# Attention scores with keys on partitions, two heads on halves of the array, no maximum, and a checked fallback

## Chip, cores, metric

One Trainium2 chip, one core. The time is device microseconds of the whole program, from the first to the last instruction; every figure called a time is a median of runs on the chip. TensorE's granted clock is told by the profile.

## The reference, cut to what matters

```python
# x: (32, 512, 512) float32, adj: (512, 512) float32 of 0 and 1, with ones on the diagonal
def L0(x, adj, Wq, bq, Wk, bk, Wv, bv):            # H = 8 heads of HD = 64
    q, k, v = [(x @ W + b).reshape(b_, n, H, HD) for W, b in ...]
    scores = einsum('bihd,bjhd->bhij', q, k) / sqrt(64)
    scores = scores + where(adj == 0, -1e9, 0)
    return einsum('bhij,bjhd->bihd', softmax(scores, axis=-1), v)
def L1(x, adj, weight, bias):                      # d = rsqrt of the degrees
    return einsum('nm,bmo->bno', adj * d[:, None] * d[None, :], x @ weight) + bias
x = layernorm(x + L0(x, ...));  x = layernorm(x + L1(x, ...))
```

So there are 32 graphs of 512 nodes, each with 8 heads. Everything stays float32.

## The kernel before

Queries and keys are made transposed, two heads in each block of 128 partitions. Scores have queries on partitions; the softmax's weights are then turned on TensorE for the product with the values. Cuts are marked.

```python
    def scores(s):
        b, i, h = s                                   # graph, 128 queries, head
        r = slice((h % 2) * HD, (h % 2 + 1) * HD)
        p = ps_sc.tile([P, N], F32, name="sc")
        nc.tensor.matmul(p, QT[b][r, h // 2, ts(i, P)], KT[b][r, h // 2, :], start=True, stop=True)
        # ... neg = -(p + mask), low = its minimum (VectorE, one instruction)
        nc.scalar.activation(E[s], neg, AF.Exp, bias=low, scale=-1.0, accum_out=SUMS[b, i][:, h : h + 1])

    def turn(s):
        for j in range(NT):
            nc.tensor.transpose(p[:, j, :], e[:, ts(j, P)], ident)
        # ... to SBUF on VectorE or ScalarE in turn

    def values(s):
        for j in range(NT):
            nc.tensor.matmul(av[:, h, :], et[:, j, :], V[b][:, j, ts(h, HD)], start=j == 0, stop=j == NT - 1)
        # ... after the last head: 1 / sums, weighting, residual, layer norm

    for k in range(S + 3):
        # ... scores(k), turn(k - 2), values(k - 3); all of project(b + 1) at once in mid-graph,
        #     all of convolve(b - 1) at once at step 8
```

`project` and `convolve` are 12 and 8 pieces a graph, each of four float32 products with 512 columns; I call these 20 the pieces.

## Time and profile before

| | before |
|---|---|
| time, median (lowest to highest) | 4829.75 us (4829.08 to 4830.41) |
| TensorE busy, granted clock | 99.6% of the span, 0.999 |
| VectorE, ScalarE, GpSimd busy | 35%, 29%, 10% |
| TensorE instructions | 19,984 matmul instructions (two to a float32 product, one to a transpose) and as many weight loads |

TensorE is busy from end to end, so time can only be won by fewer or shorter TensorE slots. A slot is the distance between starts; recorded durations overlap. The profile's lines are in the prediction below. In them PE is TensorE, PEld its weight loads, DVE VectorE, ACT ScalarE and POOL GpSimd; L157 is line 157 of the kernel; a line of the groups view ends with the busy us, the mean ns of one, and the idle us ahead of it with its cause.

### The profile page before, as it was taken

The numbers are of one execution on the slowest core, as the hardware profiler recorded it, in microseconds if no ns is written. First come the engines' busy times: TensorE is split into PE (matmuls) and PEld (weight loads), VectorE is DVE, ScalarE is ACT, GpSimd is POOL, SyncE is SP. The second block draws the span as 40 slices with busy tenths as digits, with TensorE's granted clock in tenths as the row PEclk, the third lists the DMA queues.
The fourth block names the chain that finished last, engine by engine and source line by source line (L and its number), as shares of the span: only waits on it lengthen the run. The fifth ranks groups of instructions, "written<-read, shape, count | busy, mean of one in ns | idle before, by whom it ended". The sixth has DMA issues, their size and how long they took to land.

```text
span 4827.6 us, 50352 instructions
## 1 busy us (share of the span) xinstructions
PE 4808.6 (100%) x19984; PEld 2717.6 (56%) x19984; DVE 1700.5 (35%) x4110; ACT 1402.3 (29%) x3073; POOL 462.8 (10%) x520
## 2 busy tenths in 40 slices
PE   9999999999999999999999999999999999999999
PEld 4555555555555555555555555555555555555555
DVE  2433334333343333433334333343333433334334
ACT  2232233322333222332223232232322323223232
POOL 0100101000010100101001010010000110101101
PEclk9999999999999999999999999999999999999999
DMA  1000000000000000000000000000000000000000
GB/s 66 18 10 9 18 18 18 10 9 18 18 18 9 12 16 18 18 9 18 9 18 18 9 18 9 18 18 9 18 9 18 18 9 18 9 18 18 9 9 18
DMA packets 38009, 76.10 MB, mean 16 GB/s; under 512 B 2192, under 2 KB 2192, under 8 KB 37776
## 3 DMA queue, kind: packets, MB, share of 16 engines
q1 hardware_dynamic: 37776, 72.88, 4.2%
q8 instruction: 159, 2.61, 0.2%
q14 instruction: 74, 0.61, 0.0%
HBM read 39.33 MB, written 33.55 MB: 15 GB/s over the span
## 4 chain that ended last, share of the span: by engine, by line
PE 99%; DMA 0%; DVE 0%; POOL 0%; issue 0%; SPq 0%; POOLq 0%
PE sc L157 22%; PE mm L142 18%; PE av L199 18%; PE tr L174 12%; PE mm L229 9%; PE mm L147 9%; PE mm L221 9%; PE mm L133 1%; DMA wk<-in_L_gnn_Wk_dram 0%; PE mm L122 0%; DVE st L183 0%; POOL y L210 0%; DVE y L231 0%; DVE y L207 0%; POOLq L290 0%
## 5 line engine op out<-in xcount | busy, mean ns | idle before, releaser
L157 PE MATMUL sc<-kT,qT 64*128 64x512 f32 x2048 | 1149.3, 641 | 0.0
L160 DVE CUSTOM_DVE_ANT_0 neg<-sc,mask 128x512 f32<-128x512 f32 x1024 | 707.8, 691 | 973.9 <-PE sc L157 969.1
L199 PE MATMUL av<-v,eT 128*128 128x64 f32 x8192 | 1027.4, 268 | 0.0
L199 PEld LDWEIGHTS av<-v,eT 128*128 128x128 f32 x8192 | 995.5, 192 | 1.0 <-issue 0.7
L166 ACT ACTIVATE e<-neg,low 128x512 f32<-128x512 f32 x1024 | 740.7, 723 | 767.8 <-DVE low L160 767.6
L174 PEld LDWEIGHTS tr<-ident,e 128*128 128x128 f32 x4096 | 432.9, 141 | 767.6 <-ACT e L166 655.8
L179 ACT COPY eT<-tr 128x512 f32<-128x512 f32 x512 | 299.6, 585 | 1506.9 <-PE tr L174 1506.9
L174 PE MATMUL tr<-ident,e 128*128 128x128 f32 x4096 | 675.5, 286 | 0.0
L148 DVE TENSOR_TENSOR v<-mm,bv_r 128x512 f32<-128x512 f32 x128 | 88.5, 692 | 1266.9 <-PE mm L147 1266.9
L210 POOL TENSOR_TENSOR y<-y,x 128x512 f32<-128x512 f32 x128 | 162.2, 1268 | 3293.6 <-DVE y L207 2811.6
L142 PE MATMUL mm<-xT,wk 128*128 128x512 f32 x1024 | 449.7, 597 | 3.3 <-DMA wk<-in_L_gnn_Wk_dram 2.6
L221 PE MATMUL mm<-naT,x 128*128 128x512 f32 x1024 | 447.2, 594 | 1.0 <-DVE x L190 1.0
L142 PE MATMUL mm<-xT,wq 128*128 128x512 f32 x1024 | 444.7, 592 | 0.0
L147 PE MATMUL mm<-wv,xT 128*128 128x512 f32 x1024 | 444.7, 592 | 0.0
L229 PE MATMUL mm<-w,zT 128*128 128x512 f32 x1024 | 444.7, 592 | 0.0
L157 PEld LDWEIGHTS sc<-kT,qT 64*128 64x128 f32 x2048 | 301.4, 184 | 93.7 <-issue 29.3
L177 DVE COPY eT<-tr 128x512 f32<-128x512 f32 x512 | 349.6, 683 | 2.1 <-PE tr L174 2.1
L147 PEld LDWEIGHTS mm<-wv,xT 128*128 128x128 f32 x1024 | 194.6, 190 | 244.9 <-issue 244.9
L229 PEld LDWEIGHTS mm<-w,zT 128*128 128x128 f32 x1024 | 194.6, 190 | 244.9 <-issue 244.9
L142 PEld LDWEIGHTS mm<-xT,wq 128*128 128x128 f32 x1024 | 194.6, 190 | 244.9 <-issue 244.9
L142 PEld LDWEIGHTS mm<-xT,wk 128*128 128x128 f32 x1024 | 192.5, 190 | 241.5 <-issue 225.9
L221 PEld LDWEIGHTS mm<-naT,x 128*128 128x128 f32 x1024 | 191.8, 190 | 230.2 <-issue 227.7
(37 smaller groups left out, 1649.4 us busy)
## 6 DMA issues: line engine op xcount, KB each, us to landing
x<-in_x_dram SPq DMA_DIRECT2D x32, 1024.0 KB, 5.1
out_dram<-ob SPq DMA_DIRECT2D x32, 1024.0 KB, 4.2
wq<-in_L_gnn_Wq_dram SPq DMA_DIRECT2D x1, 1024.0 KB, 7.8
wk<-in_L_gnn_Wk_dram SPq DMA_DIRECT2D x1, 1024.0 KB, 10.4
wv<-in_L_gnn_Wv_dram SPq DMA_DIRECT2D x1, 1024.0 KB, 9.5
ob<-in_adj_dram SPq DMA_DIRECT2D x1, 1024.0 KB, 8.9
w<-in_L_gnn_weight_dram SPq DMA_DIRECT2D x1, 1024.0 KB, 11.0
bv_r<-in_L_gnn_bv_dram SPq DMA_DIRECT2D x1, 256.0 KB, 7.4
```

The source lines that it names most:

```text
L142: nc.tensor.matmul(p, w[:, d, ts(o, P)], xT[:, d, :], start=d == 0, stop=d == DT - 1)
L147: nc.tensor.matmul(p, xT[:, d, ts(n, P)], wv[:, d, :], start=d == 0, stop=d == DT - 1)
L157: nc.tensor.matmul(p, QT[b][r, h // 2, ts(i, P)], KT[b][r, h // 2, :], start=True, stop=True)
L160: nc.vector.tensor_tensor_reduce(neg, p, mask[:, i, :], scale=-1.0, scalar=3.4028234663852886e38, op0=ALU.add, op1=ALU.min, accum_out=low)
L166: nc.scalar.activation(E[s], neg, AF.Exp, bias=low, scale=-1.0, accum_out=SUMS[b, i][:, h : h + 1])
L174: nc.tensor.transpose(p[:, j, :], e[:, ts(j, P)], ident)
L177: nc.vector.tensor_copy(ET[s], p)
L179: nc.scalar.copy(ET[s], p)
L199: nc.tensor.matmul(av[:, h, :], et[:, j, :], V[b][:, j, ts(h, HD)], start=j == 0, stop=j == NT - 1)
L210: nc.gpsimd.tensor_add(y, y, X[b][:, i, :])
L221: nc.tensor.matmul(p, x1[:, m, ts(d, P)], naT[:, m, :], start=m == 0, stop=m == NT - 1)
L229: nc.tensor.matmul(p, zT[:, d, ts(n, P)], w1[:, d, :], start=d == 0, stop=d == DT - 1)
```

## The change

The intent: with the keys on partitions the exponentials come out as the values product wants them, so the 4096 transposes go. The values (64 columns) become the stationary side and the weights stream 512 columns at a time. The two heads of a block are issued as neighbours, on TensorE rows 0-63 and 64-127 for the scores and on columns 0-63 and 64-127 for values and sums, so that the two halves of the array may work at once. The maximum is dropped; the mask becomes a factor of 0 or 1. A running sum of totals and reciprocals on GpSimd is tested at the end, and a complete general path stands behind a branch (not taken here). Projections and convolutions are handed out in pieces between the attention's groups. A group is two heads of a graph, all 512 queries: 128 groups, four to a graph.

```diff
-    def scores(s):
-        ...
-        nc.tensor.matmul(p, QT[b][r, h // 2, ts(i, P)], KT[b][r, h // 2, :], start=True, stop=True)
-        ... tensor_tensor_reduce (add mask, minimum), exp with bias=low and accum_out
-    def turn(s): ... (four transposes and a copy for each head and 128 queries)
+    def scores(g, j):
+        b, q = divmod(g, NP)
+        p = ps_sc.tile([P, 2, N], F32, name="sc")
+        for u in range(2):
+            r = slice(u * HD, (u + 1) * HD)
+            nc.tensor.matmul(p[:, u, :], KT[b][r, q, ts(j, P)], QT[b][r, q, :], start=True, stop=True)
+        e = work.tile([P, 2, N], F32, name="e", bufs=2 * NT)
+        nc.scalar.activation(e, p, AF.Exp, scale=SCALE)
+        nc.vector.tensor_mul(e, e, maskT[:, j, None, :].to_broadcast([P, 2, N]))
+        ... total of the four e's on VectorE
+    def values(g):
+        for j in range(NT):
+            e = E.pop((g, j))
+            for u in range(2):
+                nc.tensor.matmul(p[u * HD : (u + 1) * HD, :], V[b][:, j, ts(2 * q + u, HD)], e[:, u, :],
+                                 start=j == 0, stop=j == NT - 1)
+        for u in range(2):
+            nc.tensor.matmul(s[u * HD : (u + 1) * HD, :], ones, total[:, u, :], start=True, stop=True)
+        nc.gpsimd.tensor_add(seen_total, seen_total, total)
+        nc.vector.reciprocal(r, s)
+        nc.gpsimd.tensor_add(seen_recip, seen_recip, r)
+        nc.vector.tensor_mul(OT[g], p, r)
+    def residual(g): ... four transposes of OT[g], added to x; after the last group the layer norm
+    for g in range(G + 1):
+        ... scores(g, 0), scores(g, 1), values(g - 1), scores(g, 2), scores(g, 3)
+        for k in range(max(n_project, n_convolve)):
+            if k < n_project:
+                projecting.pop(0)()
+            if k < n_convolve:
+                convolving.pop(0)()
+        ... residual(g - 1)
```

(Cut: the general path, the mask's transposes, the layer norm over four tiles at once, the test and branch at the end.)

## The prediction

> **What bounds the kernel now.** I read the page first (busy table, chain that ended last, groups), then the timeline of TensorE over some microseconds in the middle, then the groups by line for the small VectorE operations.
>
> ```profile
> PE 4808.6 (100%) x19984; PEld 2717.6 (56%) x19984; DVE 1700.5 (35%) x4110; ACT 1402.3 (29%) x3073; POOL 462.8 (10%) x520
> ...
> PE 99%; DMA 0%; DVE 0%; POOL 0%; issue 0%; SPq 0%; POOLq 0%
> PE sc L157 22%; PE mm L142 18%; PE av L199 18%; PE tr L174 12%; PE mm L229 9%; PE mm L147 9%; PE mm L221 9%; PE mm L133 1%; DMA wk<-in_L_gnn_Wk_dram 0%; PE mm L122 0%; DVE st L183 0%; POOL y L210 0%; DVE y L231 0%; DVE y L207 0%; POOLq L290 0%
> ...
> L157 PE MATMUL sc<-kT,qT 64*128 64x512 f32 x2048 | 1149.3, 641 | 0.0
> ...
> L199 PE MATMUL av<-v,eT 128*128 128x64 f32 x8192 | 1027.4, 268 | 0.0
> ...
> L174 PE MATMUL tr<-ident,e 128*128 128x128 f32 x4096 | 675.5, 286 | 0.0
> ...
> L142 PE MATMUL mm<-xT,wq 128*128 128x512 f32 x1024 | 444.7, 592 | 0.0
> ```
>
> TensorE does everything: 99% of the chain, no idle time ahead of any matmul group. So the time is a sum of TensorE slots. One float32 product is two instructions (L142 has 512 products and 1024 instructions), and the slot of an instruction with 512 columns is 444.7/1024 = 0.434 us, although its recorded duration is 592 ns (records overlap). A product with 512 columns costs 0.868 us.
>
> The timeline gives the slots of an attention step (one head, 128 queries), from start to start:
>
> ```profile
> 2400.82 1.12 PE L157 MATMUL sc<-kT,qT 64*128 64x512 f32 x2
> 2401.88 0.66 PE L174 MATMUL tr<-ident,e 128*128 128x128 f32 x4
> 2402.37 1.00 PE L199 MATMUL av<-v,eT 128*128 128x64 f32 x8
> 2403.30 1.12 PE L157 MATMUL sc<-kT,qT 64*128 64x512 f32 x2
> ```
>
> Scores 1.06, turning the weights 0.49, values 0.93, together 2.48 us. With 1024 steps that is 2540 us; 20 pieces of projection and convolution for each of 32 graphs, 8 instructions each, are 20 x 32 x 3.47 = 2222; turning x (L133) 70. The sum is 4832 against a span of 4827.6, so this account is complete. Two things stand out. A scores product takes 1.06 us where two slots of a full product are 0.87: 0.19 us a step are lost at the change between 64 rows and 128. And the values stream 64 columns for each load of 128 weights: 0.116 us for each of 8 pairs, where 64 columns at the rate of L142 are 0.054. They are bound by weight loads.
>
> The other engines matter only for what comes after:
>
> ```profile
> L166 ACT ACTIVATE e<-neg,low 128x512 f32<-128x512 f32 x1024 | 740.7, 723 | 767.8 <-DVE low L160 767.6
> ...
> L210 POOL TENSOR_TENSOR y<-y,x 128x512 f32<-128x512 f32 x128 | 162.2, 1268 | 3293.6 <-DVE y L207 2811.6 <-issue 482.0
> L207 DVE TENSOR_TENSOR y<-av,inv 128x512 f32<-128x512 f32 x128 | 88.5, 692 | 94.3 <-PE av L199 94.3
> ...
> L222 ACT COPY zT<-mm 128x512 f32<-128x512 f32 x128 | 74.9, 585 | 381.7 <-PE mm L221 381.7
> ...
> L205 DVE RECIPROCAL inv<-sums 128x8 f32<-128x8 f32 x128 | 26.0, 203 | 35.8 <-ACT e L166 35.8
> ...
> L116 DVE TENSOR_TENSOR dis<-root,pos 128x4 f32<-128x4 f32 x1 | 0.2, 165 | 1.2 <-POOL root L114 1.2
> ```
>
> **What the Trainium skill says.** (1) "TensorEngine Tiling (Array Packing)", Key Properties: tiles of the array work independently, but changing the tiling mode drains TensorE. The trace agrees with the second half (the 0.19 us above); the first half it can't show, since no two products on different halves are neighbours in it. (2) "TensorE: Matmul & The Clock Gate", Part 3, measured speedup: four row tiles gave 3.07x and three column tiles 2.38x at 512 columns, and matmuls start and end in program order. Nothing says that this held for float32, and no trace here shows it. (3) "VectorE: DVE Perf Modes", the section on the TRN2 errata: a float32 tensor_tensor takes (N+151)/0.96 ns. For N = 512 this is 691, the trace has 692; for 1024 I get an estimate of 1.22 us. (4) "SBUF — State Buffer", Who interferes with whom: VectorE and GpSimd share a port pair as an exclusive lock. No view of before shows a case; afterwards GpSimd adds while VectorE multiplies.
>
> **The change part by part.** The unit is a group: two heads of one graph, all 512 queries; 4 groups a graph, 128 in all.
>
> Removed: all 4096 transposes of weights with their 1024 evacuations, the maximum on VectorE, and values products with only 64 columns. Now the values are the stationary side (64 columns) and the weights stream, 512 columns at a time. The count of scores products stays 1024.
>
> Scores: 8 products a group, in two bursts of four, alternately on rows 0-63 and 64-127 and into different banks. Call the instructions of a burst A1 A2 B1 B2 A1' A2' B1' B2'. As the order is kept and each half does one at a time, A2 runs beside B1, B2 beside A1' and so on: 5 slots instead of 8. With one drain at 0.19: 2 x (5 x 0.434 + 0.19) = 4.72 us.
>
> Values: 8 products on alternating column halves, then 2 products with ones that give the sums already spread over 64 partitions: 20 instructions in 11 slots: 11 x 0.434 + 0.19 = 4.96 us. (Unpaired the sums alone would cost 256 x 0.868 = 222 us.)
>
> Turning the output back: 4 transposes a group, 0.55 us (L133: 69.6/128 = 0.54). Turning x: the same, 0.55. Unchanged: 5 pieces a group, 5 x 3.47 = 17.36 us.
>
> Sum: 4.72 + 4.96 + 0.55 + 0.55 + 17.36 = 28.14 us; x 128 = **3602 us**.
>
> Beside it, for each group: ScalarE has 4 exponentials of 1024 columns, under 2 x 0.585 = 1.17 us each, and 3 evacuations of about 0.65: some 6.6 us. VectorE has 7 operations on 1024 columns (4 masks, 3 additions) x 1.22 = 8.6; a reciprocal on 512 columns; four operations of 0.69 (weighting, residual, v, convolution) = 2.8; and two layer norms a graph, 5.9 each or 2.9 a group (4 x (0.695 + 0.176 + 0.547), + 0.15). The reciprocal is slow: 203 ns for 8 elements, where an ordinary operation on 4 takes 165, or 161 without its 4 x 1.04 ns; (203 - 161)/8 = 5.25 ns an element, 512 x 5.25 + 161 = 2.85 us, which is drawn from a very small case, so 2.4 to 4.4. Sum 8.6 + 2.9 + 2.8 + 2.9 = 17.2 us, 61% of the group. GpSimd: 2.5 + 1.3 + 1.3 us, estimated from 1268 ns for 512 columns, about 5 us. Each is below TensorE, so it stays the bound on average.
>
> Waits I add. The short iteration is the first of a graph: only x is turned in it, so TensorE has 4.7 + 5.0 + 2.2 + 0.6 = 12.5 us of work, while VectorE has about 11.5 us up to the finished output of the previous group plus masks and the layer norm behind it. The transposes of x also need evacuations on ScalarE behind two exponentials. I take 1.5 us there, and 1.7 us in the later iterations where v and the convolution are evacuated behind VectorE's queue of masks: 3.2 x 32 = about 100 us. At the ends: the last group has nothing to fill its chain (sums, reciprocal, weighting, transpose, residual, layer norm, about 11 us), then comes the convolution's own norm, and the new check with its branch; before, all idle time was 19 us. I add 45. **3602 + 100 + 45 = about 3750 us.**
>
> **The rivals.** *No overlap of float32 halves.* Each product keeps 0.868: scores 2 x (4 x 0.868 + 0.19) = 7.32, values and sums 10 x 0.868 + 0.19 = 8.87, the rest 18.46: 34.65 x 128 = 4435, with about 100 for waits and ends 4540. For it: nothing here shows float32 pairs side by side. Against: row halves read disjoint partitions, and the instructions' order allows it. *Only row halves overlap* (column halves need two streams of moving data from the same partitions): 4.72 + 8.87 + 18.46 = 32.05, x 128 = 4102, with waits 4220. *Only column halves*: 7.32 + 4.96 + 18.46 = 30.74, 3935, with waits 4055. *VectorE becomes the bound*: if the shared port blocks it for the 5 us of GpSimd and the reciprocal takes 4.4, its group is 24 us, still under 28, but bursts would show: 6 to 8 us a graph, 200 us more, about 3900. *Each mode change is dearer*, as there are now about four a group: at 0.4 us each instead of 0.57 in all it would be +130 us.
>
> **Range and chances.** I give full overlap 0.65 (3600 to 3950 with its waits), row alone 0.13, column alone 0.05, none 0.12, and 0.05 to surprises such as a longer slot in tiled modes. Even without any overlap the sum is 6% below 4830, so faster by over 2% is 0.96, within 2% 0.03, slower 0.01. The range 3560 to 4240 holds full overlap and most of row overlap; the middle is the full-overlap sum.
>
> **What would show it.** Scores in the groups view: about 2 x 5 x 0.434 x 128 = 556 us of TensorE busy time (889 if not paired), and starts a few ns apart for A2 and B1. Values and sums together about 611 us (1111 if not). Pieces still 0.434 us an instruction. Exponentials near 1.1 us, masks 1.22, reciprocal 2.4 to 4.4. The chain should stay over 93% TensorE, with the rest naming VectorE in each graph's first iteration. The prediction is wrong if paired products start 0.43 us apart all through, if TensorE idles over 8% behind VectorE, or if the tiled slots are longer than 0.434.

## The result

3758.42 us (3757.99 to 3760.56, 4 runs) against 4829.75; ratio 0.7783, 95% interval 0.7772 to 0.7794. All outputs are right. Ratios are the mean time of one kernel's fast runs over that of the other's of the same rounds, so not quite the ratio of the medians quoted. The predicted 3750 is within 0.3%. The experiments show that this closeness is partly luck: two terms of the sum were off by 4 to 5 us a graph each, in opposite directions.

The page of the changed kernel, busy times first and then the groups that answer to those of before (busy us, mean ns | idle ahead of them and its cause):

```profile
PE 3537.8 (94%) x10786; PEld 1471.0 (39%) x10786; DVE 2297.7 (61%) x2390; ACT 817.7 (22%) x1025; POOL 825.8 (22%) x459
...
L294 ACT ACTIVATE e<-sc 128x1024 f32<-128x1024 f32 x512 | 499.9, 1022 | 1325.9 <-PE sc L292 1325.9
L295 DVE TENSOR_TENSOR e<-e,maskT 128x1024 f32<-128x1024 f32 x512 | 698.3, 1385 | 128.9 <-ACT e L294 128.9
L322 POOL TENSOR_TENSOR seen_recip<-seen_recip,recip 128x512 f32<-128x512 f32 x128 | 263.6, 2059 | 2091.1 <-DVE recip L321 1842.8
L363 PE MATMUL mm<-naT,x 128*128 128x512 f32 x1024 | 538.6, 676 | 185.5 <-DVE x L338 185.5
L292 PE MATMUL sc<-qT,kT 64*128 64x512 f32 x2048 | 554.1, 618 | 0.8 <-ACT e L294 0.8
L311 PE MATMUL av<-e,v 128*64 128x512 f32 x2048 | 467.7, 598 | 0.0
L321 DVE RECIPROCAL recip<-su 128x512 f32<-128x512 f32 x128 | 428.6, 3349 | 60.2 <-PE su L318 60.2
L264 PE MATMUL mm<-xT,wk 128*128 128x512 f32 x1024 | 464.9, 598 | 0.0
```

There are about half as many TensorE instructions (54%), and 2048 scores instructions of 512 columns take 554 us instead of 1149. TensorE is no longer full: one group, the convolution's gather L363, has 185.5 us of idle time ahead of it, all for VectorE's last step of the layer norm (L338); and its own instructions are busy 538.6 us where the like-sized L264 have 464.9. The chain that ended last cannot be used here: it stops at the branch at the end and names less than 1% of the span.

The timeline of TensorE shows a graph's first two groups (start us, busy us, line, how many):

```profile
2000.31 1.99 PE L292 MATMUL sc<-qT,kT 64*128 64x512 f32 x8
2002.22 3.65 PE L311 MATMUL av<-e,v 128*64 128x512 f32 x16
2005.71 1.03 PE L318 MATMUL su<-total,ones 128*64 128x512 f32 x4
...
2009.61 1.12 PE L292 MATMUL sc<-qT,kT 64*128 64x512 f32 x2
...
2020.74 3.70 PE L264 MATMUL mm<-xT,wk 128*128 128x512 f32 x8
2030.33 6.04 PE L363 MATMUL mm<-naT,x 128*128 128x512 f32 x8 [5.89 <-DVE x L338]
2036.20 3.60 PE L264 MATMUL mm<-xT,wk 128*128 128x512 f32 x8
```

From start to start a scores burst of 8 instructions takes 1.91 us and the 16 of the values 3.49, which is 8 slots of 0.436: two instructions to a slot. The starts in the trace's records say the same (us, first six instructions of the scores burst): 2000.307, 2000.314, 2000.840, 2000.847, 2001.270, 2001.276. Pairs start 7 ns apart. At 2030.33 the bracket shows the wait of 5.89 us, and the eight gather instructions after it take 5.87 us to the next start instead of 3.43. The table of stretches tells why:

```profile
2013.32:2030.33 17.01, 11.12 (x41) 3.77 (x41) 14.84 (x19) 4.20 (x5) 5.46 (x3) 0.94 0.00 0
2030.33:2036.20 5.87, 5.87 (x8) 2.56 (x9) 5.84 (x8) 0.00 (x0) 0.00 (x0) 0.60 0.00 0
2053.90:2086.84 32.94, 32.94 (x97) 13.78 (x96) 18.44 (x16) 7.21 (x10) 10.39 (x6) 1.00 0.00 0
```

Columns are the stretch, its length, busy time (count) of TensorE, weight loads, VectorE, ScalarE and GpSimd, then the granted clock, DMA share and GB/s. The clock is 0.60 in the gather after the wait, and 1.00 in a group without one. In the clock records the half-speed interval comes once in each graph that has such a wait and lasts 6.8 us.

What VectorE and GpSimd did before that gather, in the same window:

```profile
2016.34 3.07 DVE L295 TENSOR_TENSOR e<-e,maskT 128x1024 f32<-128x1024 f32 x1
...
2023.13 3.32 DVE L321 RECIPROCAL recip<-su 128x512 f32<-128x512 f32 x1
2026.37 0.10 DVE L334 TENSOR_SCALAR ve<-mv 128x4 f32<-128x4 f32 x1
...
2029.73 1.92 DVE L338 TENSOR_SCALAR x<-x,mv,rstd 128x512 f32<-128x512 f32 x4 [2.13 <-POOL rstd L336]
```

```profile
2015.96 2.36 POOL L319 TENSOR_TENSOR seen_total<-seen_total,total 128x1024 f32<-128x1024 f32 x1 [3.62 <-DVE total L301]
2026.59 2.12 POOL L322 TENSOR_TENSOR seen_recip<-seen_recip,recip 128x512 f32<-128x512 f32 x1 [8.27 <-DVE ve L334]
2028.68 1.01 POOL L336 TENSOR_TENSOR rstd<-ve,minus_half 128x4 f32<-128x4 f32 x1
```

The statistics are done by 2023.2. Then a reciprocal of the next group (3.32 us) stands ahead of `ve`, a running sum of the check (2.12 us) stands ahead of the power `rstd` on GpSimd, and a mask has taken 3.07 us instead of its usual 1.2 while GpSimd's `seen_total` ran (it ended 1.08 us after that sum did).

### The profile page after: what moved, and what is told of

Same layout as the page of the kernel before. It is cut to its first block, busy times and chain, and to the rows that moved or that the text cites. A ratio compares the mean times of both kernels' runs of the same rounds, so it can differ in the third digit from the quotient of the medians.

```text
span 3758.5 us, 26652 instructions
## 1 busy us (share of the span) xinstructions
PE 3537.8 (94%) x10786; PEld 1471.0 (39%) x10786; DVE 2297.7 (61%) x2390; ACT 817.7 (22%) x1025; POOL 825.8 (22%) x459
## 5 line engine op out<-in xcount | busy, mean ns | idle before, releaser
L294 ACT ACTIVATE e<-sc 128x1024 f32<-128x1024 f32 x512 | 499.9, 1022 | 1325.9 <-PE sc L292 1325.9
L295 DVE TENSOR_TENSOR e<-e,maskT 128x1024 f32<-128x1024 f32 x512 | 698.3, 1385 | 128.9 <-ACT e L294 128.9
L322 POOL TENSOR_TENSOR seen_recip<-seen_recip,recip 128x512 f32<-128x512 f32 x128 | 263.6, 2059 | 2091.1 <-DVE recip L321 1842.8
L363 PE MATMUL mm<-naT,x 128*128 128x512 f32 x1024 | 538.6, 676 | 185.5 <-DVE x L338 185.5
L292 PE MATMUL sc<-qT,kT 64*128 64x512 f32 x2048 | 554.1, 618 | 0.8 <-ACT e L294 0.8
L311 PE MATMUL av<-e,v 128*64 128x512 f32 x2048 | 467.7, 598 | 0.0
L321 DVE RECIPROCAL recip<-su 128x512 f32<-128x512 f32 x128 | 428.6, 3349 | 60.2 <-PE su L318 60.2
L264 PE MATMUL mm<-xT,wk 128*128 128x512 f32 x1024 | 464.9, 598 | 0.0
L264 PE MATMUL mm<-xT,wq 128*128 128x512 f32 x1024 | 462.6, 595 | 0.0
L349 DVE TENSOR_TENSOR x<-mm,x 128x512 f32<-128x512 f32 x128 | 87.9, 687 | 591.2 <-PE mm L347 591.2
L319 POOL TENSOR_TENSOR seen_total<-seen_total,total 128x1024 f32<-128x1024 f32 x128 | 302.8, 2366 | 573.0 <-DVE total L301 573.0
L363 PEld LDWEIGHTS mm<-naT,x 128*128 128x128 f32 x1024 | 221.8, 220 | 486.9 <-issue 248.9
L301 DVE TENSOR_TENSOR total<-total,e 128x1024 f32<-128x1024 f32 x256 | 387.3, 1513 | 3.2
L372 DVE TENSOR_TENSOR x<-mm,x 128x512 f32<-128x512 f32 x128 | 88.1, 688 | 411.5 <-PE mm L371 411.5
L264 PEld LDWEIGHTS mm<-xT,wk 128*128 128x128 f32 x1024 | 192.8, 191 | 255.0 <-issue 254.7
L264 PEld LDWEIGHTS mm<-xT,wq 128*128 128x128 f32 x1024 | 192.0, 190 | 253.6 <-issue 253.6
L292 PEld LDWEIGHTS sc<-qT,kT 64*128 64x128 f32 x2048 | 182.8, 185 | 244.5 <-issue 239.7
L311 PEld LDWEIGHTS av<-e,v 128*64 128x64 f32 x2048 | 135.6, 136 | 315.2 <-issue 305.0
```

The costliest lines, as they stand in the source:

```text
L264: nc.tensor.matmul(p, w[:, d, ts(o, P)], XT[b][:, d, :], start=d == 0, stop=d == DT - 1)
L292: nc.tensor.matmul(p[:, u, :], KT[b][r, q, ts(j, P)], QT[b][r, q, :], start=True, stop=True)
L294: nc.scalar.activation(e, p, AF.Exp, scale=SCALE)
L295: nc.vector.tensor_mul(e, e, maskT[:, j, None, :].to_broadcast([P, 2, N]))
L301: nc.vector.tensor_add(E[g], E[g], e)
L311: nc.tensor.matmul(p[u * HD : (u + 1) * HD, :], V[b][:, j, ts(2 * q + u, HD)], e[:, u, :], start=j == 0, stop=j == NT - 1,)
```

## The experiments

Two theories: the gain is the overlap of the array's halves, or it is the layout (no transposes, long streams). And two for what was left on the table: a fixed delay of the layer norm with too little work in front of it, or VectorE too slow in general. The times:

| run | us, median | ratio to before | us a graph (steady) |
|---|---|---|---|
| changed kernel | 3758.42 | 0.7783 | 116.05 |
| fill4 | 3502.88 | 0.7254 | 107.56 |
| lead2 | 3619.82 | 0.7494 | 110.34 or 112.04 |
| nochecks | 3601.28 | 0.7456 | 110.14 or 111.84 |
| before_nomax | 4828.45 | 0.9999 | |
| rows_apart_f | 3558.07 | 0.7367 | 109.26 |
| cols_apart_f | 3724.17 | 0.7711 | 114.63 |
| both_apart_f | 3775.32 | 0.7819 | 116.18 |
| fill4_turns | 3508.72 | 0.7265 | 107.78 |
| rows_same_f | 3903.74 | 0.8084 | 120.38 |
| cols_split_f | 4146.66 | 0.8587 | 128.02 |
| no_pairs_f | 4478.55 | 0.9274 | 138.45 |
| fill_nochecks | 3495.46 | 0.7238 | 107.56 |

The last column is the distance in the trace between the turning of x in one graph and in the next. Differences between rows of different calls are of medians; the kernel before was within 0.02% in all of them.

### fill4: other work ahead of the gather

```diff
-            if k < n_convolve:
+            if 0 <= k - lead + 1 < n_convolve:     # lead = 4 in a graph's second group, else 1
                 convolving.pop(0)()
```

> Edit: in the second group of a graph all four projection pieces come before the three gather pieces of the convolution, instead of alternating from the first on. Theory A (the wait ahead of the gather, 5.89 us a graph for the layer norm, is exposed only because too little other work stands before it, and the half clock after it is its consequence): three more pieces are 10.3 us of work, over 5.9 + the layer norm's 1.9, so both the wait and the slow gather vanish: 32 x (5.9 + 2.4) = 265 us less, about 3490 us, clock 0.99 or above, gather at 0.43 us an instruction. Theory B (VectorE is behind everywhere and the wait only moves): the wait comes back ahead of the gather or of another piece, time within 2% of 3758.

3502.88 us. Theory A holds: the steady graph is 8.49 us shorter, which is the 6.05 us that TensorE's next slot came late (counted from start to start; the 5.89 in the profile counts from the modelled end of the product before) and 2.44 of slow gather. TensorE's longest waits on VectorE in the changed kernel, then in fill4 (who waited for whom: us in total, times, longest):

```profile
PE mm L363 <- DVE x L338: 185.5, 32, 6.1
```

```profile
PE mm L347 <- DVE oT L324: 9.7, 2, 8.7
PE mm L363 <- DVE x L338: 7.4, 3, 6.1
```

and the gather's group in fill4, to be held against the 538.6 us above:

```profile
L363 PE MATMUL mm<-naT,x 128*128 128x512 f32 x1024 | 453.0, 595 | 7.4 <-DVE x L338 7.4
```

VectorE's work is unchanged, and nothing else waits longer (L347 waited 9.7 us before as well). The clock is 0.996. This version beats both kernels: 0.7254 of before, and 0.932 of the changed kernel's median.

### lead2: one piece more instead of three

The same edit with `lead = 2`.

> Edit: two projection pieces instead of one before the first gather piece. One piece more is 3.43 us, so 2.4 us of the 5.89 us wait should stay. If an idle time of 2.4 us is too short to bring the half clock, the time falls by 32 x (3.43 + 2.44) = 188 us to about 3570 and the clock is 0.99 or above; if any wait brings it, by 32 x 3.43 = 110 us to about 3648 with a clock of 0.97. If the wait is not a fixed delay of the layer norm (the norm itself moves later), less than 50 us are won.

3619.82 us, between the two figures. The wait is 2.55 us in every graph, as A says. But the half clock comes in some graphs and not in others: of the first 30 graphs' gathers after the wait, 11 spread their eight starts over 3.08 us and 19 over 4.7 us or more, and the clock records hold 19 half-speed intervals of 3.4 us in that time. So 2.55 us of idle time can bring the half clock, or not. The clock records tell the two cases apart: all half-speed intervals start on one grid of 3.413 us (two of them in lead2 lie 112.6 us apart, which is 33 steps, others 221.9, which is 65). Counted from the end of the last slot before it, the 19 waits that began between 0.5 us before and 0.3 us after a point of that grid brought one; the 11 that began 0.6 to 1.3 us before one did not. No experiment here moved the wait against the grid on purpose.

### nochecks: GpSimd's sums, the test and the general path out

```diff
-        nc.gpsimd.tensor_add(seen_total, seen_total, total)
-        nc.gpsimd.tensor_add(seen_recip, seen_recip, r)
```

> Edit: the two running sums on GpSimd, the test at the end and the general path are taken out; the result is still right on these inputs. Theory A (GpSimd's sums delay the layer norm in two ways: its power instruction queues behind a sum of 2.1 us, and VectorE's masks and totals wait for the shared port): masks fall from 1385 to about 1220 ns, totals from 1513 to about 1230, the wait ahead of the gather from 5.9 to about 3 us, and if that is short enough for the clock, 32 x (2.9 + 2.4) = 170 us less, about 3590; 90 us less if the clock still falls. Rival: the reciprocal of 3.35 us on VectorE alone makes the wait, then masks get shorter but the wait stays above 5 us and the time within 1% of 3758.

3601.28 us. The groups by line of this run:

```profile
L295 DVE TENSOR_TENSOR e<-e,maskT 128x1024 f32<-128x1024 f32 x512 | 609.4, 1211 | 128.5 <-ACT e L294 128.5
...
L361 PE MATMUL mm<-naT,x 128*128 128x512 f32 x1024 | 492.6, 628 | 77.4 <-DVE x L336 77.4
```

Masks fall from 1385 to 1211 ns and the wait from 5.89 to 2.32 us; the rival is out. The half clock comes in 15 of the first 30 graphs' gathers after the wait, and they sort on the clock's grid as in lead2 (with: from 0.4 us before a point to 0.4 after; without: 0.5 to 1.7 before). The checks cost 157 us in the changed kernel, not by their own work but by delaying a layer norm that TensorE waited for.

### fill_nochecks: the same on top of fill4

> Edit on top of fill4: the check and the general path taken out, as in nochecks. With the wait ahead of the gather filled, GpSimd's sums and the slower masks stand beside TensorE's work and cost nothing there; only the end (tests, branch, last running sum) remains: 3503 less 3 to 12 us. If the sums still cost something inside, over 30 us less.

3495.46 us, 7.4 less than fill4, and the steady graph is 107.56 us in both. With the gather's wait filled, the checks cost nothing inside; what remains is about 6 us after the start of the last graph. So the checks are nearly free once nothing waits for the layer norm behind them.

### before_nomax: one part of the change alone

```diff
-        nc.vector.tensor_tensor_reduce(neg, p, mask[:, i, :], scale=-1.0, ..., op0=ALU.add, op1=ALU.min, accum_out=low)
-        nc.scalar.activation(E[s], neg, AF.Exp, bias=low, scale=-1.0, accum_out=SUMS[b, i][:, h : h + 1])
+        nc.scalar.activation(raw, p, AF.Exp)
+        nc.vector.tensor_tensor_reduce(E[s], raw, mask[:, i, :], scale=1.0, ..., op0=ALU.mult, op1=ALU.add, accum_out=...)
```

> Edit in the kernel before the change: one part of the change alone, no maximum. ScalarE exponentiates the scores straight from the accumulators, VectorE then multiplies by a mask of 0 and 1 and sums. TensorE's instructions stay as they are. If TensorE's slots are the whole time, leaving out the maximum is worth nothing by itself: 4830 us within 0.5%. If the softmax chain set the pace anywhere, over 1% faster.

4828.45 us, ratio 0.9999 (0.9983 to 1.0016). Dropping the maximum is worth nothing alone, as TensorE was the bound. It is worth what it permits: with keys on partitions a maximum over keys would run across partitions.

### rows_apart_f, cols_apart_f, both_apart_f: the order of the halves

```diff
-    scores: A B A' B'          (A: rows 0-63, B: rows 64-127; two tiles of keys)
+    scores: A A' B B'
-    values: A B A B A B A B    (A: columns 0-63, B: columns 64-127)
+    values: A A A A B B B B
```

> Edit on top of fill4 (3503 us, no wait that could hide a change): in each burst of four scores products the two of the lower rows come first, then the two of the upper rows, so only the middle two are neighbours on different halves. Theory A (products overlap only where neighbours in program order lie on different halves): a burst has at least 6 slots (A, then A' beside B, then B': 2 + 2 + 2) and at most 7, not 4, so +2 to +3 slots x 0.434 us x 2 bursts x 128 groups = +222 to +333 us, 3725 to 3836 us. Rival (TensorE reorders products by itself as it finds a free half, or the scores gain has another cause than overlap): 4 slots as before, 3503 us within 1%.

> Edit on top of fill4: the four values products of the left column half come first, then the four of the right one; the two sums products stay neighbours. Theory A: 14 to 15 slots instead of 8, +6 to +7 slots x 0.434 x 128 = +333 to +389 us, 3836 to 3892 us, and the values group's busy time goes from 469 us to over 800. Rival (column halves do not really run side by side, or the order does not matter): 3503 us within 1%.

> Edit on top of fill4: both of the above. Theory A: the two add up, +555 to +722 us, 4058 to 4225 us; with the sums still paired (0.87 us a group) and the middle pairs still overlapping, no pairing at all would be some 250 us more, which would leave little of the gain over 4829. Rival (the new layout gains by fewer and longer instructions, not by overlap): below 3700.

My theory that only neighbours pair is wrong. In rows_apart_f a full burst takes 1.92 us as before, with pairs 13 to 14 ns apart (starts at 2002.222 and 2002.235, 2002.755 and 2002.768), although the compiled program has the order A A' B B':

```profile
2002.22 1.99 PE L293 MATMUL sc<-qT,kT 64*128 64x512 f32 x8
```

Half of the 55 us comes from a graph's first group, where the burst is torn apart between transposes, so that the two B's there stand alone (1.91 us for two products where fill4 has 1.06: 0.85 us of the 1.70 that a graph is longer). Most of the rest is in the same group, about 0.55 us, with a wait for ScalarE's copies of the turned x (0.27 us) in it. In cols_apart_f TensorE looks ahead only so far:

```profile
2031.44 4.13 PE L311 MATMUL av<-e,v 128*64 128x512 f32 x13
2034.98 0.64 PE L318 MATMUL su<-total,ones 128*64 128x512 f32 x1
2035.41 0.59 PE L311 MATMUL av<-e,v 128*64 128x512 f32 x1
```

A sums product (L318) starts at 2034.98, ahead of the values instructions (L311) of 2035.41 and 2035.84 that come before it in the program: it is on the left half, and they are on the right half. In the starts of such a burst the first two A's run alone (0, 0.480, 0.909, 1.339 us); then the third A and the first B start together (1.768 and 1.774). So a B two products further on is reached, and one three further on is not. The measured cost, 221 us, is 7.07 us a graph, or 1.77 a group: four slots of 0.434. both_apart_f is about the sum of the two (272 us against 55 + 221).

These runs do not take the overlap away, so they do not settle what it is worth. The next three do.

### rows_same_f, cols_split_f, no_pairs_f: no partner within reach

```diff
-            r = slice(u * HD, (u + 1) * HD)                      # rows_same_f: heads 0 and 2, then 1 and 3
+            r = slice((q % 2) * HD, (q % 2 + 1) * HD)            # of two blocks: both on the same rows
-        values(g - 1)                                            # cols_split_f: one column half before
+        values(g - 1, 0); scores(g, 2); scores(g, 3); values(g - 1, 1)   # the second burst, one after it
```

no_pairs_f has both.

> Edit on top of fill4: a group takes heads 0 and 2 (or 1 and 3) of two blocks instead of 0 and 1 of one block, so both of its scores products stand on the same 64 rows; counts, sizes and everything else stay. The earlier order test failed because TensorE pairs products two places apart by itself; here no product on the other rows is within reach. If overlap of row halves is what makes a burst 1.92 us, a burst has 8 slots and not 4: 4 x 0.434 x 2 x 128 = 444 us more, 3947 us, and the scores group goes from 554 to about 1000 us busy. If the burst is short for another reason, 3503 us within 1%.

> Edit on top of fill4: the values and sum of the left column half before the second scores burst, those of the right half after it, so that no product on the other column half is within reach. If column halves overlap, values and sums take 20 slots and not 10: 10 x 0.434 x 128 = 556 us more, plus one more change of tiling mode a group at 0.1 to 0.2 us (13 to 26 us) and some wait for the later reciprocal: 4070 to 4110 us. If they do not, under 3560.

> Edit on top of fill4: both of the above, the new layout without any overlap in the array. Theory (nearly the whole gain is overlap): 3503 + 444 + 570 to 600 = 4517 to 4550 us, so the layout by itself is worth 6% and the overlap the rest. Rival (the layout gains by longer streams for each weight load and the overlap is a bonus): below 4200.

All three come out close to what overlap predicts: +401 us for the rows, +644 for the columns, +976 together, over fill4. None is exactly as stated (3904 for 3947, 4147 for 4070 to 4110, 4479 for 4517 to 4550, so about 1% off), and all are far from the rivals' 3503, 3560 and 4200. TensorE's scores and values groups in no_pairs_f, from the groups by line:

```profile
L293 PE MATMUL sc<-qT,kT 64*128 64x512 f32 x2048 | 962.9, 605 | 0.0
L315 PE MATMUL av<-e,v 128*64 128x512 f32 x2048 | 931.8, 598 | 0.4 <-DVE oT L332 0.4
```

and its timeline of a group, to be held against the one of the changed kernel:

```profile
2026.02 3.70 PE L293 MATMUL sc<-qT,kT 64*128 64x512 f32 x8
2029.64 3.65 PE L315 MATMUL av<-e,v 128*64 128x512 f32 x8
2033.13 1.02 PE L320 MATMUL su<-total,ones 128*64 128x512 f32 x2
```

The same 8 scores instructions take 3.62 us instead of 1.91, and 3.49 us now hold 8 values instructions and not 16. Rows lose less than the 444 us expected, since in fill4 some products are unpaired already (fill4_turns, below). The columns lose 88 us more than 10 slots a group (556): 60 us are new waits of TensorE ahead of v's pieces (29.2 us in that run's list of waits) and of the output's transposes (31.2), and the other 28 us, 0.22 a group, would fit one more change of tiling mode (of the rows and columns that a product uses), which was not tested. The waits are gone in no_pairs_f, which is most of why the two (1045 us) do not add up to 976.

### fill4_turns: can the torn burst be mended?

In a graph's first group single scores products of the next group stand between the transposes of x (1.06 us each, at 2009.61 above): the order was not in the source but came from the schedule that the framework makes when it lowers the program.

```diff
+        if q == 0 and projecting:      # two of the four turning pieces ahead of values(g - 1)
+            projecting.pop(0)(); projecting.pop(0)()
```

> Edit on top of fill4: in a graph's first group two of the four pieces that turn x go ahead of the values, so that the scheduler no longer puts single scores products between the transposes. In fill4 four products of the next group take three slots of 1.06 us there (1.06 + 1.06 + 1.06) where two pairs would take two: about 1.06 us less a graph, minus one or two more changes of tiling mode at 0.1 to 0.2 us: 32 x 0.8 = 25 us less, about 3478. If unpaired products cost nothing, 3503 within 0.2%.

3508.72 us, no gain (5.8 more than fill4). The pairs were mended, but the transposes of the output now came too early:

```profile
2090.37 1.13 PE L292 MATMUL sc<-qT,kT 64*128 64x512 f32 x4
2092.72 0.63 PE L347 MATMUL mm<-ident,oT 128*128 128x128 f32 x4 [1.22 <-DVE oT L324]
```

The wait for VectorE's reciprocal and weighting (1.22 us a graph) took back what the pair had saved. The single products had been filling that time.

## Why the prediction was right, and where it was not

**Bound.** TensorE stays the bound: no step of mine there failed. fill4 is 99% TensorE.

**Terms of the sum**, per graph, from the starts in the timeline of one steady graph of the changed kernel (2000.31 to 2116.36):

| term | predicted us | measured us |
|---|---|---|
| scores | 18.9 | 16.6 |
| values and sums | 19.8 | 17.8 |
| turning output and x | 4.4 | 4.2 |
| 20 pieces | 69.4 | 69.0 |
| waits and slow clock | 3.2 | 8.5 |
| sum | 115.8 | 116.1 |

Times 32, with ends of 45 (predicted) and 44.8 us (3758.4 - 32 x 116.05), this is the whole time.

**Overlap: right in mechanism, mis-sized.** The step "A2 runs beside B1: 5 slots instead of 8" failed. Both halves start together, 7 ns apart, so a burst of 8 instructions has 4 slots, and values with sums have 10, not 11. That is 8 x (2.36 - 1.92) + 4 x (4.96 - 4.45) = about 5.5 us a graph too many on my side; the torn burst in the first group gives back 1.2 us of it (16.6 - 8 x 1.92). The reason I gave, that order is kept, was also wrong: TensorE takes a product for the free half from up to two products further on. The sign "scores 556 us busy" came true (554.1) without its reason: with 5 slots predicted and 4 measured, the rest of the busy time is the tail of each burst's last record and the torn bursts; from start to start scores take 32 x 16.6 = 531 us.

**Waits: the right kind, the wrong place and size.** I put them on x's transposes and on evacuations behind VectorE: in the list of what TensorE's products waited for, neither has over 1 us in all, but for the first transpose's wait for its data. The step that failed is "3.2 x 32 = about 100 us": I had the layer norm in the first iteration's VectorE queue, but did not follow it to the first consumer, the gather, through three engines. It measured 6.05 us of wait, and 2.44 more because TensorE's clock halves after it, a term that I did not have.

**Other engines.** Exponentials took 1022 ns (under 1170 predicted), the reciprocal 3349 (2850, with 2400 to 4400 allowed), masks 1385 (1220 without interference, as nochecks shows with 1211; the rest is GpSimd's additions, see the last section), VectorE 17.9 us a group (17.2). Here the estimates held. GpSimd took 6.5 us a group and not 5: its running sum of reciprocals took 2059 ns where 1268 was assumed, and this sum stands in the layer norm's way.

**Rivals.** "No overlap" was put at 4435 us and 4540 with waits; no_pairs_f, which waits at its ends alone, is 4479. "Only row halves" (4102 before waits) and "only column halves" (3935) fit cols_split_f (4147) and rows_same_f (3904), in which just that overlap is left. "VectorE's bursts, 6 to 8 us a graph" came nearest to the missing part: the wait with its slow clock was 8.49 us a graph, 272 us in all. "Each mode change is dearer" is out: a burst has 0.18 us beyond its slots, 0.19 before. Slots of products on halves are 0.43 us too (starts at 2000.840 and 2001.270 above), so "longer slots in tiled modes" is out.

**What the change is made of.** Of the 1327 us between before and fill4, 976 is overlap of halves (no_pairs_f to fill4). The other 351 (before to no_pairs_f) is all else together, which I call layout: transposes gone, longer streams, other work in other places; only the maximum was tested apart, and it is worth nothing alone. The changed kernel as given loses 256 of this to one wait and the slow clock after it.

## What to carry to other kernels

When two heads or two blocks use half of the array's rows or columns, place their products next to each other, or at most two apart: float32 halves then run at the same time, and here this was three quarters of the gain. After such a cut look at TensorE's first wait, not at average shares: follow each small chain (statistics, power, scale) through all engines to its consumer, count the time from its producer, and put at least that much independent work before the consumer. Here TensorE also came back at half clock after every wait of 5.89 us and after half or more of those of 2.3 to 2.6 us. A total that agrees can hide two errors; check the terms.

## What the Trainium skill lacked or had wrong

- "TensorE: Matmul & The Clock Gate", Part 3 (The mechanism) says matmuls start and end in strict program order. Here starts are out of order between halves: a sums product started at 2034.98, values instructions ahead of it in the program at 2035.41 and 2035.84 (cols_apart_f), and A A' B B' ran as two pairs (rows_apart_f). The page has no reach; here a product two further on was taken and one three further on was not.
- The same part gives about 4 ns between tiles and no float32 case. Float32 pairs start 7 ns apart; a scores burst fell from 3.62 to 1.91 us (1.9x), and column pairs doubled (8 or 16 instructions in 3.49 us).
- The same page, Part 1, puts the fall to half clock at an idle window of about 3.4 us. Idle times of 2.55 us brought it in 19 graphs of 30 (lead2) and of 2.32 us in 15 of 30 (nochecks); the 30 of 1.22 us in fill4_turns brought none. Which ones did went with where the wait began on the 3.413 us grid of the clock's changes (see lead2). Intervals at half speed were 3.4 us after those and 6.8 us after idle times of 5.89.
- "TensorEngine Tiling (Array Packing)", Key Properties, says a mode change drains TensorE but not how much: 1.91 us for four slots of 0.434 leaves about 0.18 us for a scores burst, and 4.45 us for ten slots 0.11 for values with sums.
- "VectorE: DVE Perf Modes" has no time for the reciprocal: 3349 ns for 128x512 from accumulators, against 0.69 us for an addition of that size.
- "SBUF — State Buffer", Who interferes with whom, was neither lacking nor wrong: its exclusive lock holds here. In the changed kernel 63 of the 512 masks took over 1.3 us (up to 3.39); all 63 began while GpSimd did an addition and ended 1.08 to 1.09 us after it, and none of the other 449 (1.20 us on average) began so. The running sum of 512 columns took 2059 ns on average, against 1268 for a GpSimd addition of that size in the kernel before.
